# A hand-planned hybrid transformer block: new durations and ranks in the plan, and the gene norms of six batches turned by VectorE and a DRAM trip

## The chip, the core and the metric

The kernel runs on one core of a Trainium2 chip. The metric is the device time of one execution in microseconds (us). TensorE is called PE in the profile, with PEld for its weight loads; VectorE is DVE, ScalarE is ACT, GpSimd is POOL, and SyncE is SP, which here does nothing but issue DMAs. A profiled execution's span is the time from its first to its last instruction.

## The reference

Eight sequences (batches) of 256 tokens with 256 channels, all fp32, go through four residual layers, each after a layer norm:

```python
x = x + attn_a(_layernorm(x), Wqkv, Wout)          # 16 heads of 128, softmax over 256 keys
x = x + ffn(_layernorm(x), Wc, temperature, genes, Wd, Wu, norm_w, scale)
x = x + attn_b(_layernorm(x), w_q, w_k, w_v, w_o)  # 16 heads of 16, rope, block mask, causal
x = x + ffn(_layernorm(x), ...)                    # the same weights again

def ffn(x):
    xn = x * rsqrt(mean(x * x) + eps) * norm_w
    logits = einsum('btd,gd->btg', xn, Wc) / clip(temperature, 0.1)   # 512 genes
    top_vals, top_idx = top_k(logits, 32)
    expr_w = softmax(top_vals)
    expressed = einsum('btk,btkc->btc', expr_w, genes[top_idx])       # 32 wide
    down = tanh(expressed @ Wd.T); up = expressed @ Wu.T
    return down * xn * up * scale
```

The two `ffn` layers are called gene layers here.

## The kernel before

**Tiles and layers.** A batch is two tiles of 128 tokens, `xs[b, t]`, that stay in SBUF from the load to the store. The work of a batch is: attention A (`attn_a`, heads in pairs), layer 0 (the first gene layer, `ffn`), layer 1 (block attention, `attn_b`, one tile after the other), layer 2 (the second gene layer). Batch 7 takes attention A tile by tile (`attn_a_by_tile`) and its gene layers one tile at a time; the other batches run a gene layer for both tiles together. The batches do not depend on each other: while one batch is in its later layers, the next is in attention A.

**The plan.** No loop sets the order of instructions. Each operation is written down with `do(engine, (occ, lat), fn, pri, reads, writes, bufs)`: the time in ns for which it occupies its engine (`occ`), the time until its result is there (`lat`), a priority, the keys that it reads and writes, and the buffers that it holds. `Plan.order` (from line 135) then simulates the five engines: again and again it takes, of each engine, the operation with the smallest priority among those that can start within `WAIT[engine]` ns of the earliest one, and of these the one that starts first. The result is a static order for each engine, which the chip follows; real waits are by semaphores. In this simulation `HOP` is added where a result goes to another operation, `LOAD` more where PE reads it, `DRAIN` is in the latency of matmuls, and a DMA lands `FLIGHT` ns after its share of the queue, which is its size by `RATE` or `SCATTER`. A buffer comes free `HOP` ns after its last use. Where producer and user are on the same engine (SP excepted), the user may start when the producer's `occ` is over. `keep_warm` afterwards puts filler transposes into PE's gaps of more than 800 ns (line 1392 in the profile).

**Priorities.** Attention A of batch b has priorities from b to b + 1 (head by head; -0.5 for the norm on PE). For the other layers two tables hold a number for each batch, layer and tile: `PE_RANK` for PE and `EW_RANK` for VectorE, ScalarE, GpSimd and SP. A number such as 7.03 stands in the midst of batch 7's attention A; one of 20 and more is behind all of it; a negative one is ahead of all.

**Two ways to turn a matrix.** TensorE transposes 128 x 128 with the identity into a PSUM bank, and ScalarE copies the bank to SBUF. `turn` does it without these two: VectorE transposes 32 x 32 blocks into a tile `T` (line 510), SP writes `T` to a DRAM buffer `D` in four DMAs, and reads it back rearranged: with `flat=True` in four writes of 128-byte pieces (line 516) and four reads (line 526), otherwise four writes (line 519) and one read (line 528). The softmax weights of A (`PT`, used by the matmuls of line 721) and the A norms of batches 1 to 7 (`AxT`) go that way.

**The gene layer.** `ffn` calls `experts` for each tile: `normed` (statistics and scaling of the row, VectorE lines 461, 464 and 480, GpSimd lines 470 and 475) gives `Fxn`; two TensorE transposes (line 1054) and a ScalarE copy (line 1060) give `FxT`; the logits come from line 1068; four rounds of `max` (line 1078) and `match_replace` (line 1095) on VectorE mark the 32 largest; line 1100 makes the weights `Fe`, which are turned (by `turn` for batches 0 to 4, by TensorE at line 966 for the rest), multiplied with the genes (line 992) and with Wd and Wu (line 1012), and gated (lines 1025 to 1041). In `attn_b`, `Rxn` is turned at line 1134, line 1152 makes queries and keys, line 1228 scores, lines 1344 to 1361 softmax, line 1253 turns weights for batch 7, line 1292 multiplies with the values, line 1327 projects, and line 1334 adds to x. Tile 1 needs the keys and values of tile 0.

Of the kernel before, what the change touches and what calls it, by code (L numbers as in the profile page):

```python
# [16 lines left out]
B, S, DIM = 8, 256, 256  # L17
P = 128
# [14 lines left out]
    [[-0.88, -0.88], [-0.87, -0.87], [-0.86, -0.86]],  # L33
    [[-0.85, -0.85], [-0.84, -0.84], [-0.83, -0.83]],
    [[-0.82, -0.82], [7.03, -0.81], [8.72, -0.8]],
    [[7.78, -0.79], [8.7, -0.78], [7.32, -0.77]],
]
EW_RANK = [
    [[1.62, 1.49], [20.64, 2.07], [2.72, 20.2]],
    [[2.79, 3.31], [3.38, 3.19], [21.34, 1.84]],  # L40
    [[22, 4.66], [21.53, 22.1], [3.28, 4.32]],
    [[22.77, 23], [4.69, 23.1], [5.73, 23.2]],
    [[24.18, 5.62], [4.78, 23.98], [6.79, 4.31]],
    [[25.44, 6.57], [5.62, 7.27], [25.2, 7.37]],
    [[8.15, 6.17], [7.09, 26.01], [29.52, 26.55]],
    [[9.27, 8.68], [26.56, 26.64], [7.38, 9.82]],
]
# [25 lines left out]
class Plan:  # L73
# [3 lines left out]

    HOP = 65.0
    LOAD = 300.0
    DRAIN = 165.0  # L80
    FLIGHT = 2000.0
    RATE = 330.0
    SCATTER = 200.0
    OPEN = 8
    WAIT = {"PE": 50.0, "DVE": 50.0, "ACT": 100.0, "POOL": 200.0, "SP": 400.0}

# [42 lines left out]
    def order(self):  # L129
# [31 lines left out]
        while len(done) < len(self.ops):  # L161
# [26 lines left out]
            if o.eng == "SP":  # L188
                self.moved = max(self.moved, t) + o.lat
                end = self.moved + self.FLIGHT  # L190
                open_.append(end + self.HOP)
                open_.pop(0)
            else:
                end = t + o.lat
            for b in o.bufs:
                b.touch -= 1
                b.end = max(b.end, end)
                if not b.touch:
                    slots[b.tag].append((b.end + self.HOP, b.i))
                    self.taken.setdefault((b.tag, b.i), []).append((b.begin, b.end + self.HOP))  # L200
            for u in o.users:
                u = self.ops[u]
                same = u.eng == o.eng and o.eng != "SP"
                hop = self.HOP + (self.LOAD if u.eng == "PE" else 0.0)
                u.ready = max(u.ready, t + o.occ if same else end + hop)
                u.left -= 1
                if not u.left:
                    ready[u.eng].append(u)
# [30 lines left out]
def kernel(  # L239
# [44 lines left out]
    def dve(cols, half=False):  # L284
        occ = 70.0 + cols * (0.52 if half else 1.04)
        return occ, occ + 90.0

    def act(cols, ptr=False):
        occ = 60.0 + cols * 0.833 + (90.0 if ptr else 0.0)
        return occ, occ + 110.0  # L290

# [161 lines left out]
    def normed(b, t, who, ew, rms=False, xn=None, after=(), held=()):  # L453
# [6 lines left out]
        do(  # L460
            "DVE", (330, 420), lambda: [nc.vector.bn_stats(st(), x())],
            ew, [(x, 0), *((y, 0) for y in after)], [(st, 0)],
        )
        do("DVE", (90, 175), lambda: [nc.vector.bn_aggr(mv(), st())], ew, [(st, 0)], [(mv, 0)])


        m, a = (1.0 + RMS_EPS, LN_EPS * RMS_EPS) if rms else (1.0, LN_EPS)
        do(
            "POOL", (220, 270),
            lambda: [nc.gpsimd.tensor_scalar(rs(), mv()[:, 1:2], m, a, ALU.mult, ALU.add)],  # L470
            ew, [(mv, 0)], [(rs, 0)],
        )
        do(
            "POOL", (520, 560),
            lambda: [nc.gpsimd.tensor_tensor(rs(), rs(), mhalf, ALU.pow)],
# [18 lines left out]
    def turn(sources, dst, n, pri, keys, flat=False):  # L494
# [8 lines left out]
        for j, (p, view) in enumerate(sources):  # L503
            def out(j=j):
                t = T()[:, : 4 * w].rearrange("p (c h f) -> p h c f", c=4, h=len(sources))[:, j]
                return t

            do(
                "DVE", dve(n * P),
                lambda out=out, view=view: [nc.vector.transpose(*view(out()))],  # L510
                pri, [(q, 0) for q, _ in sources], [(T, j)],
            )
# [20 lines left out]
    def normed_a(b):  # L533
# [35 lines left out]
        if b:  # L569
            for i, (a_, b_, f_) in enumerate((  # L570
# [3 lines left out]
                do(  # L574
                    "POOL", (480.0, 530.0),
                    lambda i=i, a_=a_, b_=b_, f_=f_: [
# [319 lines left out]
    def softmax(sc, keys, p, n, k, who, ew):  # L896
# [9 lines left out]
        for i in range(n):  # L906
            do(
                "ACT", (155 + k * 0.83 + 92, 155 + k * 0.83 + 200),
                lambda i=i: [nc.scalar.activation(  # L909
                    p()[:, i, :], s3()[:, i, :], AF.Exp, bias=nm()[:, i : i + 1],  # L910
                    accum_out=sm()[:, i : i + 1])],
                ew, [*keys, (nm, 0)], [(p, ("e", i)), (sm, i)],
            )
        do(
            "DVE", (75, 165), lambda: [nc.vector.reciprocal(sm(), sm())],  # L915
            ew, [], [(sm, i) for i in range(n)],
# [20 lines left out]
    def ffn(b, ts_, layer):  # L937
# [7 lines left out]
        sms = [sb([P, 1], "Fsm", 6) for _ in ts_]  # L945
        for t, xn, e, sm in zip(ts_, xns, es, sms):
            experts(
                b, t, layer, lambda stage, t=t: pe(stage, t), xn, e, sm, xns, es, [xs[b, i] for i in ts_])
        away = n == 2 and b < B - 3
# [45 lines left out]

        cost = 730.0 if n == 2 else 505.0
        do(
# [10 lines left out]
        m = P // n  # L1008
        cost = 1140.0 if n == 2 else 858.0
        do(  # L1010
# [10 lines left out]
    def gated(b, t, ew, pg, down, up, xn, sm):  # L1021
# [6 lines left out]
        do(  # L1028
            "DVE", (390, 490),
            lambda: [nc.vector.scalar_tensor_tensor(  # L1030
# [3 lines left out]
        vec(  # L1034
            b, t, 256, (700, 740),
            lambda e: [e.tensor_tensor(up(), up(), down(), ALU.mult)],
            ew, [(down, 0)], [(up, 0)],
        )
        vec(
            b, t, 256, (690, 730),  # L1040
            lambda e: [e.tensor_tensor(x(), x(), up(), ALU.add)],
            ew, [(up, 0)], [(x, 0)],
        )

    def experts(b, t, layer, pe, xn, e, sm, xns, es, both):


        ew = first(b, t, layer)
        normed(b, t, "F", ew, True, xn, both, xns)
        xT = sb([P, DC, P], "FxT", 2)  # L1050
        pt = bank("B")
        do(
            "PE", (218.0, 218.0 + plan.DRAIN),
            lambda: (nc.tensor.transpose(pt()[:, ts(c, P)], xn()[:, ts(c, P)], ident)
                     for c in range(DC)),
            pe(0), [(xn, 0)], [(pt, 0)], [xT, *es],
        )
        do(
            "ACT", act(256),
            lambda: [nc.scalar.copy(xT().rearrange("p c q -> p (c q)"), pt()[:, :S])],  # L1060
            ew, [(pt, 0)], [(xT, 0)],
        )
        pl = bank("B")
        left = sb([P, G], "Fleft", 2)
        for c in range(DC):
            do(
                "PE", mm(512),
                lambda c=c: [nc.tensor.matmul(  # L1068
                    pl(), xT()[:, c, :], wcT[:, c, :], start=c == 0, stop=c == DC - 1)],
                pe(1), [(xT, 0), ("wcT",)], [(pl, 0)], [left, *es],  # L1070
            )
        m8 = [sb([P, 8], f"Fm8{r}", 2) for r in range(4)]
        nm = sb([P, 1], "Fnm", 2)
        for r in range(4):
            src, key = (pl, (pl, 0)) if r == 0 else (left, (left, 0))
            do(
                "DVE", (600 if r else 640, 740 if r else 760),
                lambda r=r, src=src: [nc.vector.max(m8[r](), src())],  # L1078
                ew, [key], [(m8[r], 0)],
            )  # L1080
            if r == 0:
                do(
                    "DVE", (55, 150),
                    lambda: [nc.vector.tensor_scalar(
# [3 lines left out]
                do(  # L1088
                    "ACT", (690, 800),
                    lambda: [nc.scalar.activation(e(), pl(), AF.Exp, bias=nm(), scale=rtemp)],  # L1090
                    ew, [(pl, 0), (nm, 0), ("rtemp",)], [(e, 0)],
                )
            do(
                "DVE", (672, 755),
                lambda r=r, src=src: [nc.vector.match_replace(left(), m8[r](), src(), TAKEN)],  # L1095
                ew, [(m8[r], 0), key], [(left, 0)],
            )
        do(
            "DVE", (720, 820),
            lambda: [nc.vector.scalar_tensor_tensor(  # L1100
                e(), left(), TAKEN, e(), ALU.is_equal, ALU.mult, accum_out=sm())],
            ew, [(left, 0)], [(e, 0), (sm, 0)],
        )
        do("DVE", (75, 165), lambda: [nc.vector.reciprocal(sm(), sm())], ew, [], [(sm, 0)])

# [14 lines left out]
    def attn_b(b, t):  # L1120
# [26 lines left out]
        for i, n in enumerate("qk"):  # L1147
# [11 lines left out]
        do(  # L1159
            "DVE", (620, 720),  # L1160
            lambda: [nc.vector.stream_shuffle(sh().rearrange("p c s -> p (c s)"), pq(), swap)],
# [9 lines left out]
        vec(  # L1171
            b, t, 512, (1235, 1280),
            lambda e: [e.tensor_tensor(
# [4 lines left out]
        vec(  # L1178
            b, t, 512, (1230, 1275),
            lambda e: [e.tensor_tensor(r(), r(), sh(), ALU.add)],  # L1180
# [3 lines left out]
        for par in range(2):  # L1184
            vec(
                b, t, 256, (460, 520),
                lambda e, par=par: [e.tensor_scalar(
# [25 lines left out]
        def scores(c, pT):  # L1213
# [7 lines left out]
            def emit():  # L1221
# [10 lines left out]
            do(  # L1232
                "PE", (1200.0, 1200.0 + plan.DRAIN), emit, pe(3),
                [(r, 0), *((kbuf, (tt, par)) for tt in range(t + 1) for par in range(2))],
# [3 lines left out]
            for g in range(NR):  # L1238
                sc, p = scs[g], ps_[g]
                do(  # L1240
                    "DVE", (n * 53 + 93, n * 53 + 180),
                    lambda sc=sc: [nc.vector.memset(
# [37 lines left out]
        def attend(cs_, pT):  # L1280
# [16 lines left out]

            cost = 1200.0 if n * len(cs_) == 2 else 650.0
            do(
# [38 lines left out]
    def softmax_b(sc, p, p3, n, k, ew):  # L1338
# [8 lines left out]
        for i in range(n):  # L1347
            do(
                "ACT", (155 + k * 0.83 + 92, 155 + k * 0.83 + 200),
                lambda i=i: [nc.scalar.activation(  # L1350
# [4 lines left out]
        do(  # L1355
            "DVE", (75, 165), lambda: [nc.vector.reciprocal(sm(), sm())],  # L1356
            ew, [], [(sm, i) for i in range(n)],
# [91 lines left out]
```

## Time and profile before

| | before |
|---|---|
| median of 3 runs | 959.45 us (958.21 to 959.88) |
| profiled execution | 960.78 us |
| its span | 959.0 us |
| first PE matmul starts | 5.0 us after the span's start |
| last PE matmul ends | 954.3 us |
| DVE busy 60 to 840 us | 594.86 us of 780 |
| DMA share of the span | 49.2% (queue of SP) |
| last attention A projection (line 876) starts | 881.9 us |

"Busy" is time in which an engine ran an instruction; matmuls are pipelined, so a busy PE is not PE at its peak. The idle time before an instruction is put down to what released it last.

The DMA issues of the two ways of `turn`, with KB each and the median us from issue to landing, are in the same part of the page as these lines:

```profile
D<-T SPq DMA_DIRECT2D x28, 64.0 KB, 3.1
AxT<-D SPq DMA_DIRECT2D x28, 64.0 KB, 2.2
```

### The profile page before, as it was taken

The page shows a single profiled execution, that of the slowest core. Times are in us where ns is not written, and L with a number is a line of the kernel's source. Part 1 is how long each engine was busy: PE and PEld are TensorE (multiplying, and loading weights), DVE is VectorE, ACT ScalarE, POOL GpSimd, SP SyncE. Part 2 cuts the span into 40 slices and gives each one's busy share as a digit, 9 for nine tenths or more (in the row PEclk, how much of TensorE's full clock was granted, in tenths as well). Part 3 has the DMA queues.
Part 4 walks back from the last instruction along what each step waited for, and adds up shares of the span by engine and source line. Part 5 has one row for each costly group of instructions (what it writes and reads, how often), then busy time and mean ns, then how long its engine had stood idle before and what let it go on. Part 6 is the DMA issues. An engine that isn't in the chain of part 4 may idle for free.

```text
span 959.0 us, 17226 instructions
## 1 busy us (share of the span) xinstructions
PE 919.5 (96%) x5815; PEld 737.7 (77%) x5815; DVE 703.6 (73%) x1716; ACT 468.0 (49%) x1550; POOL 404.4 (42%) x530
## 2 busy tenths in 40 slices
PE   7999999999999999999999999999999999999776
PEld 6878888887678777887678788877777877787564
DVE  2543484769967789669886884988788788868765
ACT  3534343754266544564455554465436643764461
POOL 4722224642176422662247343464237414743430
PEclk9999999999999999999999999999999999999989
DMA  9873333476337763485455746177525731550000
GB/s 324 248 209 94 110 106 115 123 221 173 111 111 200 202 166 105 131 231 174 135 143 171 200 133 190 44 208 216 148 67 163 211 106 40 147 173 1 6 7 12
DMA packets 109192, 136.09 MB, mean 142 GB/s; under 512 B 26288, under 2 KB 90416, under 8 KB 109104
## 3 DMA queue, kind: packets, MB, share of 16 engines
q1 hardware_dynamic: 109104, 134.99, 49.2%
q8 instruction: 46, 0.75, 0.3%
q14 instruction: 42, 0.34, 0.1%
HBM read 72.82 MB, written 62.13 MB: 141 GB/s over the span
## 4 chain that ended last, share of the span: by engine, by line
PE 56%; DVE 32%; issue 4%; DMA 3%; POOL 2%; ACT 2%; SPq 1%; DVEq 0%; ACTq 0%
PE ps L674 12%; DVE Fleft L1095 8%; DVE Fm L1078 7%; PE ps L696 7%; PE ps L721 6%; PE ps L595 5%; PE ps L743 5%; DVE T L510 4%; PE ps L1068 2%; PE ps L1228 2%; DMA D<-T 2%; PE ps L1152 2%; DVE Bnm L1344 2%; DVE Fe L1100 2%; PE ps L789 2%
## 5 line engine op out<-in xcount | busy, mean ns | idle before, releaser
L920 POOL TENSOR_TENSOR p<-p,Asm 128x512 f32<-128x512 f32 x128 | 135.1, 1058 | 266.0 <-DVE Asm L915 262.7
L674 PE MATMUL ps<-AxT,wqk 128*128 128x256 f32 x896 | 222.6, 382 | 0.2 <-ACT Fe L1090 0.2
L674 PEld LDWEIGHTS ps<-AxT,wqk 128*128 128x128 f32 x896 | 169.9, 191 | 26.6 <-issue 3.5
L909 ACT ACTIVATE p<-ps,Anm 128x256 f32<-128x256 f32 x256 | 119.5, 474 | 106.7 <-DVE Anm L903 97.1
L510 DVE STREAM_TRANSPOSE T<-p 128x512 f32<-128x512 f32 x202 | 133.4, 689 | 11.6 <-POOL p L920 7.6
L1361 POOL TENSOR_TENSOR p<-p,Bsm 128x512 f32<-128x512 f32 x96 | 99.1, 1047 | 84.6 <-DVE Bsm L1356 84.1
L903 DVE TENSOR_REDUCE Anm<-ps 128x2 f32<-128x512 f32 x128 | 86.4, 678 | 52.0 <-PE ps L696 49.3
L696 PE MATMUL ps<-Aqk 128*128 128x256 f32 x448 | 119.6, 382 | 1.4 <-ACT Aqk L683 0.9
L1350 ACT ACTIVATE p<-ps,Bnm 128x128 f32<-128x128 f32 (+1 forms) x256 | 105.4, 445 | 30.9 <-DVE Bnm L1344 23.5
L743 PE MATMUL ps<-woutT,Aao 128*128 128x256 f32 x448 | 111.0, 383 | 1.4 <-ACT Aao L731 1.0
L721 PE MATMUL ps<-PT,Av 128*128 128x256 f32 x448 | 108.5, 382 | 0.2 <-DMA PT<-D 0.2
L683 ACT ACTIVATE Aqk<-ps 128x512 f32<-128x512 f32 x112 | 66.9, 605 | 69.1 <-PE ps L674 68.5
L743 PEld LDWEIGHTS ps<-woutT,Aao 128*128 128x128 f32 x448 | 82.9, 190 | 21.7 <-issue 6.6
L721 PEld LDWEIGHTS ps<-PT,Av 128*128 128x128 f32 x448 | 83.7, 190 | 17.3 <-issue 4.3
L696 PEld LDWEIGHTS ps<-Aqk 128*128 128x128 f32 x448 | 83.1, 190 | 17.3 <-ACT Aqk L683 3.6
L595 PE MATMUL ps<-wv,Ax 128*128 128x256 f32 x224 | 66.7, 386 | 2.6 <-ACT Av L616 1.8
L1344 DVE TENSOR_REDUCE Bnm<-ps 128x2 f32<-128x512 f32 (+1 forms) x96 | 66.2, 690 | 2.7
L1078 DVE MAX8 Fm<-Fleft 128x8 f32<-128x512 f32 x96 | 66.4, 692 | 2.4
L1095 DVE MATCH_REPLACE8 Fleft<-Fm,Fleft 128x512 f32<-128x512 f32 x96 | 64.8, 675 | 0.0
L616 ACT COPY Av<-ps 128x256 f32<-128x256 f32 x108 | 40.6, 376 | 46.8 <-PE ps L595 46.5
L1068 PE MATMUL ps<-wcT,FxT 128*128 128x512 f32 x128 | 60.8, 601 | 0.0
L1350 ACT ACTIVATION_READ_ACCUMULATOR p<-ps,Bnm 128x1 f32 x256 | 58.6, 229 | 0.0
(130 smaller groups left out, 1405.6 us busy)
## 6 DMA issues: line engine op xcount, KB each, us to landing
D<-T SPq DMA_DIRECT2D x444, 128.0 KB, 2.6
PT<-D SPq DMA_DIRECT2D x111, 512.0 KB, 4.1
wqk<-in_wqkvT_dram SPq DMA_DIRECT2D x8, 512.0 KB, 9.7
x<-in_x_dram SPq DMA_DIRECT2D x16, 128.0 KB, 3.4
wv<-in_wqkvT_dram SPq DMA_DIRECT2D x4, 512.0 KB, 10.0
woutT<-in_woutT_dram SPq DMA_DIRECT2D x4, 512.0 KB, 10.6
out_dram<-x SPq DMA_DIRECT2D x16, 128.0 KB, 2.0
D<-T SPq DMA_DIRECT2D x28, 64.0 KB, 3.1
```

Of the source, the lines that this page charges most:

```text
L510: lambda out=out, view=view: [nc.vector.transpose(*view(out()))],
L595: lambda: [nc.tensor.matmul(dst(), a(), w_, start=start, stop=True, skip_group_check=not start)],
L674: lambda kind=kind, c=c: [nc.tensor.matmul(pq()[:, ts(kind, S)].rearrange("p (t q) -> p t q", t=TT), wA[kind, g][:, c, ts(i, DA)], xT.row( ...
L696: lambda t=t: [nc.tensor.matmul(sc()[:, ts(t, S)], qk()[:, 0, ts(t, P)], qk()[:, 1, :], start=True, stop=True)],
L721: lambda j=j, k=k, g=g, i=i: [nc.tensor.matmul(po()[:, ts(j, S)].rearrange("p (t g q) -> p t g q", t=TT, g=4), vs[g]()[:, AT[k, i // 2], t ...
L743: lambda t=t, h=h: [nc.tensor.matmul(py()[:, ts(t, DIM)], ao[h - h % 2]()[:, h % 2, ts(t, P)], woutT[:, h, :], start=h == hs[0], stop=h == ...
L909: lambda i=i: [nc.scalar.activation(p()[:, i, :], s3()[:, i, :], AF.Exp, bias=nm()[:, i : i + 1], accum_out=sm()[:, i : i + 1])],
L920: lambda: [nc.gpsimd.tensor_tensor(p(), p(), sm().unsqueeze(2).to_broadcast((P, n, k)), ALU.mult)],
L1078: lambda r=r, src=src: [nc.vector.max(m8[r](), src())],
L1095: lambda r=r, src=src: [nc.vector.match_replace(left(), m8[r](), src(), TAKEN)],
L1350: lambda i=i: [nc.scalar.activation(p3()[:, i, :], s3()[:, i, :], AF.Exp, bias=nm()[:, i : i + 1], accum_out=sm()[:, i : i + 1])],
L1361: lambda: [nc.gpsimd.tensor_tensor(p3(), p3(), sm().unsqueeze(2).to_broadcast((P, n, k)), ALU.mult)],
```

## The change

There are three parts. The plan's durations are replaced nearly throughout; the rule for a user on the producer's own engine now holds for PE alone, so that on the other engines it waits for the producer's end and a hop; `HOP` becomes a number for each engine, `FREE` takes its place where a buffer comes free, and `WAIT` becomes 1 ns for all but VectorE. Both rank tables are new in many places. And in `ffn`, for batches 0 to 5, both tiles are normed first and then turned together by `turn(..., flat=True)` into one buffer `FxT` of both tiles, in place of the TensorE transposes and ScalarE copies; batches 6 and 7 keep those. What is computed stays the same.

```diff
-    [[-0.85, -0.85], [-0.84, -0.84], [-0.83, -0.83]],
-    [[-0.82, -0.82], [7.03, -0.81], [8.72, -0.8]],
-    [[7.78, -0.79], [8.7, -0.78], [7.32, -0.77]],
+    [[-0.85, -0.85], [-0.84, -0.84], [7.63, 6.56]],
+    [[-0.82, -0.82], [-0.81, -0.81], [7.18, 8.48]],
+    [[-0.79, -0.79], [-0.78, -0.78], [9.75, 7.16]],
 ]
 EW_RANK = [
-    [[1.62, 1.49], [20.64, 2.07], [2.72, 20.2]],
+    [[20, 20], [1.14, 1.45], [0.24, 20.2]],
...
-    [[8.15, 6.17], [7.09, 26.01], [29.52, 26.55]],
-    [[9.27, 8.68], [26.56, 26.64], [7.38, 9.82]],
+    [[9, 26], [7.22, 26.1], [26.23, 8.63]],
+    [[27, 9.22], [7.63, 8.46], [9.27, 8.63]],
...
-    HOP = 65.0
-    LOAD = 300.0
+    HOP = {"PE": 60.0, "DVE": 35.0, "ACT": 60.0, "POOL": 79.0, "SP": 60.0}
+    FREE = 40.0
+    LOAD = 200.0
     DRAIN = 165.0
-    FLIGHT = 2000.0
+    FLIGHT = 1600.0
     RATE = 330.0
-    SCATTER = 200.0
+    SCATTER = 290.0
     OPEN = 8
-    WAIT = {"PE": 50.0, "DVE": 50.0, "ACT": 100.0, "POOL": 200.0, "SP": 400.0}
+    WAIT = {"PE": 1.0, "DVE": 100.0, "ACT": 1.0, "POOL": 1.0, "SP": 1.0}
...
-                same = u.eng == o.eng and o.eng != "SP"
-                hop = self.HOP + (self.LOAD if u.eng == "PE" else 0.0)
+                same = u.eng == o.eng == "PE"
+                hop = self.HOP[u.eng] + (self.LOAD if u.eng == "PE" else 0.0)
                 u.ready = max(u.ready, t + o.occ if same else end + hop)
...
     def dve(cols, half=False):
-        occ = 70.0 + cols * (0.52 if half else 1.04)
-        return occ, occ + 90.0
+        occ = 65.0 + cols * (0.52 if half else 1.04)
+        return occ, occ + 78.0
...
-        for t, xn, e, sm in zip(ts_, xns, es, sms):
+        by_trip = n == 2 and b < B - 2
+        xT = sb([P, TT, S], "FxT", 1)
+        for t, xn in zip(ts_, xns):
+            normed(b, t, "F", first(b, t, layer), True, xn, [xs[b, i] for i in ts_], xns)
+        if by_trip:
+            turn(
+                [(xn, lambda T, xn=xn: (
+                    T.rearrange("p c (k q) -> p k c q", k=DC),
+                    xn().rearrange("p (k c q) -> p k c q", k=DC, c=4))) for xn in xns],
+                lambda: xT().rearrange("p t s -> p (t s)"), DC, first(b, ts_[-1], layer),
+                [(xT, i) for i in range(n)], flat=True,
+            )
+        else:
+            for i, (t, xn) in enumerate(zip(ts_, xns)):
+                pt = bank("B")
+                do(
+                    "PE", (218.0, 218.0 + plan.DRAIN),
...
+                    pe(0, t), [(xn, 0)], [(pt, 0)], [xT, *es],
+                )
...
+        for i, (t, xn, e, sm) in enumerate(zip(ts_, xns, es, sms)):
             experts(
-                b, t, layer, lambda stage, t=t: pe(stage, t), xn, e, sm, xns, es, [xs[b, i] for i in ts_])
+                b, t, layer, lambda stage, t=t: pe(stage, t), (xT, i), lambda c, i=i: xT()[:, i, ts(c, P)], e, sm, es)
...
             do(
-                "DVE", (600 if r else 640, 740 if r else 760),
+                "DVE", (610, 690),
                 lambda r=r, src=src: [nc.vector.max(m8[r](), src())],
...
             do(
-                "DVE", (672, 755),
+                "DVE", (671, 753),
                 lambda r=r, src=src: [nc.vector.match_replace(left(), m8[r](), src(), TAKEN)],
```

The remaining lines of the diff replace further durations in the same manner, most by a few per cent.

## The prediction

> **What bounds the kernel now.** I read the page's busy shares first, then busy time by stage, then PE's own waits, then the chain of waits near the end, then the DMA issues.
>
> ```profile
> span 959.0 us, 17226 instructions
> PE 919.5 (96%) x5815; PEld 737.7 (77%) x5815; DVE 703.6 (73%) x1716; ACT 468.0 (49%) x1550; POOL 404.4 (42%) x530
> ```
>
> ```profile
> 60.00:840.00 780.00, 766.83 (x4763) 617.46 (x4762) 594.86 (x1439) 387.52 (x1300) 330.00 (x421) 1.00 0.52 148
> 840.00:900.00 60.00, 55.71 (x433) 43.56 (x434) 48.14 (x124) 28.46 (x86) 22.81 (x30) 1.00 0.22 65
> 900.00:959.00 59.00, 42.16 (x394) 32.27 (x392) 35.69 (x92) 26.26 (x91) 17.34 (x22) 0.92 0.03 10
> ```
>
> Columns of the second fence: stage, length, then busy time (instructions) of PE, PEld, DVE, ACT and POOL, the granted clock, DMA share, GB/s. TensorE sets the pace of the body: from 60 to 840 us it idles 780 - 766.83 = 13.2 us, at a granted clock of 1.00. VectorE is the next engine, at 594.86 / 780 = 76%. In the last 119 us PE idles 4.3 + 16.8 = 21.1 us, and 149 of its instructions there are fillers (line 1392), so the end is a chain and not a full engine.
>
> ```profile
> PE ps L966 <- DVE Fe L1100: 7.1, 8, 2.2
> PE ps L1134 <- DVE Rxn L480: 4.5, 5, 2.1
> PE ps L1054 <- DVE Fxn L480: 3.2, 4, 1.4
> PE ps L1253 <- POOL p L1361: 3.2, 4, 2.0
> PE ps L721 <- DMA PT<-D: 0.2, 1, 0.2
> ```
>
> These are PE's waits over the whole span (total, times, longest). They are for the ends of VectorE's chains; for a DRAM trip's landing PE waits 0.2 us in all. The DMA-queue trips therefore cost nothing today, and the transposes on PE do.
>
> **The change part by part.** I sum against the span of 959.0 us. The profiled execution took 960.78 us, 1.78 above its span; the median of the runs, 959.45, stands 0.45 above the span, and I add that at the end.
>
> *(a) 48 transposes leave PE.* Six batches (0 to 5), two gene layers, two tiles, two 128-column transposes each. A pair costs PE the step from its start to the next instruction's:
>
> ```profile
> 328.23 0.38 PE L1054 MATMUL ps<-ident,Fxn 128*128 128x128 f32 x2
> 328.45 1.03 PE L721 MATMUL ps<-PT,Av 128*128 128x256 f32 x4
> ```
>
> 0.22 us for two, so 24 pairs x 0.22 = 5.3 us off a full engine. The waits in front of them go too: 0.8 us from 60 to 840 us (PE's idle time there before line 1054 that Fxn ended). I take -6.1; the bounds are -6.1 and 0 (the freed time becomes a wait elsewhere). ScalarE loses 24 copies of 0.38 us (line 1060), and 24 uses of a PSUM bank go with them; at 49% busy ScalarE sets nothing, so I cost that at nothing.
>
> *(b) Twelve DRAM trips come instead.* Each is two VectorE transposes, four writes and four reads on SP's queue, the way that the A norms already go. VectorE: 24 x 0.419 us (the mean of the 14 transposes T<-Axn) = 10.1 us, which raises its share by one point; PE's work covers it, and if that cover is gone it is at most +10.1 on the end. SP: each write is in the queue 0.63 us and each read 0.42 us (medians of lines 516 and 526), 48 x 0.63 + 48 x 0.42 = 50 us over the first 800 or so. All SP issues now add up to about 305 us of 959, so the queue has room; but it is in order, and reads of PT for heads stand behind a write that waits on VectorE (205 us of SP's waits are of that kind). The latency of a trip rises: from the start of the first T<-Axn to the last landing I read 8.6 to 13.2 us in three A trips, against 0.22 + 0.38 us of work through PE. What covers it is the next batch's A heads, which do not need this batch's gene result. With it hidden I take 0; the bounds are 0 and 12 x 1.05 = +12.6 (the mean of the four waits of VectorE for a T buffer, 4.2 us in all, paid once by each trip).
>
> The Trainium skill, page "VectorE: DVE Perf Modes", section "Rules for kernel authors", speaks against this part: for a full 128x128 transpose it names TensorE where a PSUM destination is acceptable, since VectorE turns only 32x32 blocks. The rows above agree on latency, 0.6 us of work against some 9 us of trip; by that rule taken as a cost on the path, the sum would be 12 x 8 = 96 us worse, and by the rows, which show a busy PE and no PE wait for trips, 6.1 us better.
>
> *(c) The plan's durations.* The static order is made from these numbers. One step matters most: before, an operation on the same engine could follow when the producer's slot ended; now it waits for the result and a hop. The trace, in the chain of waits:
>
> ```profile
> 876.44 0.70 DVE Fm L1078
> 877.17 0.76 DVE Fleft L1095 x2
> 877.96 0.71 DVE Fm L1078
> ```
>
> A round of top-k takes 877.96 - 876.44 = 1.52 us. The old plan allowed 0.640 + 0.672 = 1.31, the new one 0.690 + 0.035 + 0.753 + 0.035 = 1.51. Over four rounds the old plan had the result Fe some 0.8 us too early, and PE's largest wait is for Fe (7.1 us, 8 times). So the old order puts PE at such places before the data; the new one would fill in other work first. At most the whole idle time of the body goes, 13.2 us less the 0.8 of (a) = 12.4; at least none. As the greatest named waits are of this kind but not all, I take about half, -6.4.
>
> *(d) The plan's DMA times go the other way.* Page rows:
>
> ```profile
> D<-T SPq DMA_DIRECT2D x444, 128.0 KB, 2.6
> PT<-D SPq DMA_DIRECT2D x111, 512.0 KB, 4.1
> ```
>
> Four writes are issued within 1.31 us (the median from first to fourth), so an undisturbed head trip takes 1.31 + 2.6 + 4.1 = 8.0 us. The old constants give 4 x 0.655 + 2.0, a hop of 0.065, then 2.62 + 2.0 = 9.3 us. The new give 4 x 0.452 + 1.6, a hop of 0.06, then 1.81 + 1.6 = 6.9 us: 1.1 short of the trace, and 2.4 us earlier than the old plan. PE's load margin falls by 0.1 as well. So PE meets its L721 matmuls 2.5 us earlier relative to the landing. For the 56 head pairs before, I took the time from the last landing of a PT read to the pair's first L721 matmul: median 3.0 us, lower quartile 1.6. In 22 of the 56 it is under 2.5, and the shortfalls add up to 26.9 us. That is the upper bound; the lower is 0. A wait of PE delays all that follows and so gives the other trips in flight their time back, and SP, whose window of choice goes from 400 to 1 ns, should send reads with fewer detours (a read now issues 5.8 us after its first write by the median, though the writes have landed after 4.2). I take a quarter, +6.7.
>
> *(e) The end.* Batch 7's block attention gets ranks 7.63 and 8.46 where it had 26.56 and 26.64, so it goes ahead of batch 6's last gene layer (tile 0 26.23 and tile 1 8.63, before 29.52 and 26.55). On the chain of waits the top-k of one such tile lies from 872.69 to 880.29 us, 7.6 us. I take half of it, -4; the bounds are -8 (all of it) and +10 (rival 3).
>
> The other parts (the ranks of early batches, FREE, POOL's costs) change the order where PE is full either way, and have no row of their own; they are inside (c). One buffer FxT for both tiles in place of two half as large costs nothing where gene layers lie apart: pairs of Fxn stand 10 us and more apart, and a tile needs it some 3 us until its logits.
>
> Sum: 959.0 - 6.1 + 0 - 6.4 + 6.7 - 4 = 949.2; plus 0.45 = 949.7, so **950 us**.
>
> **The rivals.** 1. *Only the transposes count*: PE gains (a) and the rest cancels, 959.0 - 6.1 + 0.45 = 953.4. For it: PE is full, and its body floor hardly moves. Against: six named waits that the durations speak to.
>
> 2. *The trips are counted too short, and PE waits for landings* (slower): the wait that is 0.2 us now takes the place of those removed, at line 721. Price: all of 26.9 us, against gains of (a) and (c): 959.0 - 6.1 - 6.4 + 26.9 + 0.45 = 973.9. It decides from where more than 6.1 + 6.4 = 12.5 us are paid, about half. For it: the plan's own 6.9 against 8.0 us. Against: waits in a pipeline of several trips are not added up one by one.
>
> 3. *The end is late* (slower): batch 7's first gene layer of tile 0 gets rank 27, behind everything else on VectorE, and tile 1's block attention needs that tile's keys. If its top-k (7.6 us) and the norm, reciprocal and gating around it (some 2.4 us by rows of 0.16 to 0.48) fall behind the last A head, the end moves by +10; with the rest of (c) and (d) at their values, 949.2 + 4 + 10 + 0.45 = 963.7. Against: VectorE idles 60 - 48.1 = 11.9 us from 840 to 900, where such low work still finds its place.
>
> 4. *No change*: gains and the DMA shortfall cancel within 0.2%, 1.9 us (about what a measurement of this kernel can tell from no change).
>
> **How the numbers follow.** Chances: the forecast 0.46, rival 1 0.17, rival 2 0.20, rival 3 0.11, no change 0.06. Faster 0.46 + 0.17 = 0.63, same 0.06, slower 0.31. The forecast's own range goes from all of (a), (c) and the end's -8 with no DMA wait, 959.0 - 6.1 - 12.4 - 8 + 0.45 = 933, to 956. The range of 8 in 10 adds rival 3 and the lower half of rival 2: 933 to 970.
>
> **What would show it.** Right: no L1054 matmul for batches 0 to 5 (16 left of 64), 24 more T transposes of 128x256, PE waits on Fe, Rxn and Fxn in the body under 6 us, PE's idle time from 60 to 840 at 7 to 14 us, part of it now on landings of PT or FxT. Rival 2: waits of PE or PEld for PT<-D or FxT<-D of over 12 us in all. Rival 3: the top-k of batch 7's first layer, tile 0, after the last L876. The prediction is wrong if VectorE, not PE, is full in the body (over 85% from 60 to 840), or if the time from the last L876 to the end is over 90 us (77 now).

## The result

The changed kernel takes 989.29 us (median of 4 runs, 986.16 to 989.67) against 958.83 us for the kernel before in the same comparison: a ratio of 1.0309, 95% interval 1.0286 to 1.0333, so 3.1% slower. The forecast was 950 us. The profiled execution took 989.36 us with a span of 987.6 us, 28.6 us more than the 959.0 before.

### The profile page after: what moved, and what is told of

Read it like the earlier page. It is cut to its first block, busy times and chain, and to the rows that moved or that the text cites. A ratio compares the mean times of both kernels' runs of the same rounds, so it can differ in the third digit from the quotient of the medians.

```text
span 987.6 us, 17304 instructions
## 1 busy us (share of the span) xinstructions
PE 921.5 (93%) x5748; PEld 731.3 (74%) x5748; DVE 685.7 (69%) x1740; ACT 462.2 (47%) x1526; POOL 403.5 (41%) x530
## 2 busy tenths in 40 slices
DMA packets 136841, 142.38 MB, mean 144 GB/s; under 512 B 52401, under 2 KB 116529, under 8 KB 136753
## 3 DMA queue, kind: packets, MB, share of 16 engines
q1 hardware_dynamic: 136752, 141.29, 50.7%
## 4 chain that ended last, share of the span: by engine, by line
PE 42%; DMA 21%; DVE 19%; SPq 7%; issue 4%; ACT 3%; POOL 3%; DVEq 0%; ACTq 0%; POOLq 0%
DMA PT<-D 10%; DMA D<-T 9%; PE ps L675 7%; PE ps L744 5%; PE ps L722 5%; SPq L520 4%; PE ps L1082 4%; DVE T L511 4%; PE ps L697 4%; DVE Fleft L1109 4%; PE ps L596 3%; DVE Fm L1092 3%; PE ps L1166 2%; DMA FxT<-D 2%; DVE Anm L904 1%
## 5 line engine op out<-in xcount | busy, mean ns | idle before, releaser
L722 PE MATMUL ps<-PT,Av 128*128 128x256 f32 x448 | 112.9, 392 | 18.1 <-DMA PT<-D 16.6
L697 PEld LDWEIGHTS ps<-Aqk 128*128 128x128 f32 x448 | 83.9, 190 | 16.4 <-issue 4.3
L732 ACT COPY Aao<-ps 128x512 f32<-128x512 f32 x56 | 33.0, 593 | 76.8 <-PE ps L722 76.4
L1092 DVE MAX8 Fm<-Fleft 128x8 f32<-128x512 f32 x96 | 64.2, 683 | 0.5
L1358 DVE TENSOR_REDUCE Bnm<-ps 128x2 f32<-128x512 f32 (+1 forms) x96 | 62.2, 665 | 0.1
```

Source lines behind the costliest of these rows:

```text
L697: lambda t=t: [nc.tensor.matmul(sc()[:, ts(t, S)], qk()[:, 0, ts(t, P)], qk()[:, 1, :], start=True, stop=True)],
L722: lambda j=j, k=k, g=g, i=i: [nc.tensor.matmul(po()[:, ts(j, S)].rearrange("p (t g q) -> p t g q", t=TT, g=4), vs[g]()[:, AT[k, i // 2], t ...
```

## The profile after

The page's busy shares, and then busy time by stage (stage, length, PE, PEld, DVE, ACT, POOL, clock, DMA share, GB/s):

```profile
span 987.6 us, 17304 instructions
PE 921.5 (93%) x5748; PEld 731.3 (74%) x5748; DVE 685.7 (69%) x1740; ACT 462.2 (47%) x1526; POOL 403.5 (41%) x530
...
PE 42%; DMA 21%; DVE 19%; SPq 7%; issue 4%; ACT 3%; POOL 3%; DVEq 0%; ACTq 0%; POOLq 0%
```

```profile
60.00:840.00 780.00, 735.80 (x4395) 584.50 (x4393) 546.34 (x1371) 359.83 (x1194) 303.74 (x391) 0.99 0.54 150
840.00:900.00 60.00, 59.40 (x462) 50.55 (x462) 45.49 (x121) 37.37 (x130) 34.29 (x41) 1.00 0.29 85
900.00:987.60 87.60, 71.93 (x667) 52.56 (x665) 67.77 (x185) 40.04 (x131) 32.35 (x43) 0.99 0.12 36
```

From 60 to 840 us PE now idles 780 - 735.8 = 44.2 us, where it idled 13.2. PE's idle time in the whole span grew from 39.5 to 66.1 us, by 26.6 of the 28.6. The granted clock is hardly the cause: over the whole span it is 0.994, where it was 0.995. The last line of the first fence is the chain of waits by engine: DMA has 21% of it and SP's queue 7%, where they had 3% and 1% in the same line of the kernel before:

```profile
PE 56%; DVE 32%; issue 4%; DMA 3%; POOL 2%; ACT 2%; SPq 1%; DVEq 0%; ACTq 0%
```

PE's waits by what ended them (total, times, longest) say which transfers:

```profile
PE ps L722 <- DMA PT<-D: 16.6, 19, 2.1
PE ps L1082 <- DMA FxT<-D: 8.9, 8, 2.7
PE ps L1306 <- DMA PT<-D: 8.1, 10, 1.8
PE ps L1020 <- DMA PT<-D: 5.1, 5, 1.8
...
PE ps L965 <- DVE Fxn L481: 1.9, 3, 0.7
...
PE ps L994 <- DVE Fe L1114: 1.4, 2, 1.0
```

Lines 722, 1306, 1020 and 1082 of the changed kernel are the value matmuls of attention A, those of block attention, the gene sums and the logits (before: 721, 1292, 992 and 1068). PE waited 0.2 us in all for landings before; now the first four lines alone make 38.7 us, and with a wait of 0.6 at line 860 it is 39.3. The waits for the ends of VectorE's chains went the other way: Fe 7.1 to 1.4 us, Fxn 3.2 to 1.9. The transfers themselves are hardly slower: writes of 128 KB land after 2.8 us in place of 2.6, those of 64 KB after 2.3 in place of 3.1.

```profile
D<-T SPq DMA_DIRECT2D x444, 128.0 KB, 2.8
PT<-D SPq DMA_DIRECT2D x111, 512.0 KB, 4.1
D<-T SPq DMA_DIRECT2D x76, 64.0 KB, 2.3
...
FxT<-D SPq DMA_DIRECT2D x48, 64.0 KB, 2.3
```

PT lands 4.1 us after its issue, as before, and a PT trip from the first write's issue to the landing of the read takes 9.3 us by the median (9.8 before). What changed is where PE stands in its program when the data land. From the landing of a head pair's own PT read to the first matmul of its values there were 3.4 us by the median before, and under 2.5 in 15 of the 56 pairs; now it is 0.2 us, and under 2.5 in 51. (The prediction measured from the latest landing of any PT read, which is often another pair's; by that the median before was 3.0.)

## The experiments

The theory after the result (L): the plan counts trips too short, so the order puts PE at its reads before the landings, and PE pays. Rivals: the new order (ranks, greedy choice) is bad by itself (O); VectorE's waits for a free T tile drive it (T; 4.2 us before, 37.5 now); the trip of the gene norms is the cost (D). The wait that T means is, in the changed kernel:

```profile
DVE T L511 <- DMA D<-T: 37.5, 24, 4.0
```

### 1. The same order without the waits

`after_no_landing_wait` keeps the order of the instructions of the changed kernel and takes PE's reason to wait away: the matmuls read a constant. (Dots mark lines left out; batch 7's attention A has the same replacement.)

```diff
+    still = woutT[:, :HG, :].rearrange("p h m -> p (h m)")
...
-                            pT().rearrange("p h f -> p (h f)").rearrange(
+                            still.rearrange(
                                 "p (g h k t q) -> p h k t g q", g=4, h=2, k=TT, t=TT)[:, j, k],
...
-                return wT().rearrange("p h f -> p (h f)").rearrange(
+                return still.rearrange(
...
-            return pT[g // 2]().rearrange("p h f -> p (h f)").rearrange(
+            return still.rearrange(
...
-                b, t, layer, lambda stage, t=t: pe(stage, t), (xT, i), lambda c, i=i: xT()[:, i, ts(c, P)], e, sm, es)
+                b, t, layer, lambda stage, t=t: pe(stage, t), (xT, i), lambda c, i=i: still[:, ds(i * S + c * P, P)] if by_trip else xT()[:, i, ts(c, P)], e, sm, es)
```

> The order of every engine's instructions is that of the changed kernel; only the matmuls that read a turned matrix which came back by a DRAM trip (PT of attention A, of the gene weights and of block attention, and FxT of batches 0 to 5) read the constant weights woutT instead, so TensorE never waits for these landings (the trips still run; the result leaves out what they bring). Theory L (the plan counts trips too short and PE pays the landings, 16.6 + 8.9 + 8.1 + 5.1 = 38.7 us of waits in the changed kernel): 945 to 960 us. Rival O (the new order is worse by itself: ranks, greedy choice, and the waits on landings only stand where others would): 975 to 989 us. Rival T (VectorE's waits for a free T tile, 37.5 us, drive it): 970 to 985 us, and these waits stay.

Measured: 948.15 us, ratio 0.988 (0.986 to 0.9899) to the kernel before; the span is 947.6 us, 40.0 less than that of the changed kernel. In this trace 34 of the 56 head pairs start their value matmuls before their own PT has landed, by up to 3.6 us; the median pair starts 0.5 us before. The control makes the same replacement in the kernel before:

> Control: the same replacement in the kernel before, whose PE waits for trips' landings are 0.2 us at line 721 and little elsewhere (the trips still run; the result leaves out what they bring). Theory L: 955 to 960 us, as before. If it falls by more than 1%, the replacement itself makes the kernel faster and the other run can't be read as the price of landings.

Measured: 959.92 us, ratio 1.0002 (0.9993 to 1.0012). So the replacement by itself is worth nothing in the kernel before, and the waits for landings cost the changed kernel 40 us; without them its order is 1.2% faster than the one before. The replacement has one more effect: SP may refill a PT tile without waiting for the matmuls that read it. SP's waits for PE at the PT reads are 7.4 us in the changed kernel and 11.2 in the kernel before, where taking them away gained nothing, so this is hardly the 40 us. Of these 40 us, 28.2 are idle time of PE (66.1 to 37.9 us) and 11.8 busy time (921.5 to 909.7); what makes up the second part was not traced. Rival O falls. Rival T falls too: the wait of VectorE for a T tile grew from 37.5 us to this, while the time fell:

```profile
DVE T L511 <- DMA D<-T: 46.0, 27, 4.0
```

### 2. Part of the waits

`after_A_only` makes the replacement for attention A alone, `after_FxT_only` for the logits alone.

> The changed kernel's order; only attention A's value matmuls (batches 0 to 7 where the weights came by a trip) read the constant woutT in place of PT, so that PE's waits for these landings (16.6 us at line 722) are gone and the others (FxT 8.9, block attention 8.1, genes 5.1) stay. Theory L with waits that add up: about 987.6 - 17 = 971 us of span, 968 to 975 in time. Rival (the waits absorb each other, so that the others grow into the room): 978 to 988 us, with FxT and the other PT waits over 28 us in sum, against 22.1 now.

Measured: 975.0 us (ratio 1.0152, 1.0136 to 1.0167), 14.3 less than the changed kernel; the profiled execution, the fastest of four, has a span of 971.2, 16.4 less. The 16.6 us of waits at line 722 are gone. The other landing waits grew from 22.1 us to 30.5, which is the rival's sign (over 28), but the time did not stay at the rival's 978 to 988:

```profile
PE ps L1306 <- DMA PT<-D: 14.8, 14, 2.9
PE ps L1082 <- DMA FxT<-D: 9.2, 7, 2.0
PE ps L1020 <- DMA PT<-D: 6.5, 6, 1.6
```

> The changed kernel's order; only the logits of batches 0 to 5 read the constant woutT in place of FxT (the logits are not the reference's there), so PE does not wait for the new trips of this change. Theory L, waits add up: 987.6 - 8.9 in span, 977 to 982 us in time. If the trips of this change were the main cause: 950 to 965 us. If absorbed: 985 to 989 us.

Measured: 979.56 us (1.0211, 1.0194 to 1.0228), 9.7 less than the changed kernel for 8.9 us of removed waits; the profiled execution, again the fastest of four, has a span of 974.9, 12.7 less. Attention A's waits stay (18.0 us at line 722). The waits for the trips that this change added are thus a quarter to a third of the 40 us; the rest is at trips that were there before. By the medians, each removal shortens the time by about the waits that it removes. The two add up to 24 of the 41 us between the medians of the changed kernel and of `after_no_landing_wait`; block attention and the gene weights, with 13.2 us of waits, were not tried by themselves.

### 3. One number of the plan

```diff
-    FLIGHT = 1600.0
+    FLIGHT = 2400.0
```

> The changed kernel with one number changed: FLIGHT 2400 in place of 1600, so that the plan counts a head's trip as 4 x 0.45 + 2.4 + 0.06 + 1.81 + 2.4 = 8.5 us (8.0 by the undisturbed rows of the trace). The order is a new one, with the ranks as they are. Theory L: PE's waits for landings fall from 38.7 us to under 8 and the time to 945 to 965 us, below the kernel before if the ranks still suit. Rival O (ranks and greedy choice are at fault): 970 us or more with few landing waits.

Measured: 947.25 us, ratio 0.9867 (0.9852 to 0.9881), span 946.9: as fast as the order without waits, with all work done. PE's landing waits are 9.2 us in all, a little more than the 8 that were expected:

```profile
PE ps L722 <- DMA PT<-D: 7.4, 6, 2.3
...
PE ps L1082 <- DMA FxT<-D: 1.0, 2, 0.7
...
PE ps L1306 <- DMA PT<-D: 0.6, 2, 0.3
```

The reverse, two numbers of the change in the kernel before:

```diff
-    FLIGHT = 2000.0
+    FLIGHT = 1600.0
...
-    SCATTER = 200.0
+    SCATTER = 290.0
```

> The kernel before with two numbers of the change alone: FLIGHT 1600 and SCATTER 290. Theory L: PE's waits for landings, 2 us at most before, rise to 15 us or more (no FxT trips here) and the time to 975 to 1000 us. Rival: it stays at 960 to 972, as for the order that came of a 50 ns change (971.7), with under 5 us of landing waits.

Measured in one run: 1003.92 us, more than the range given. There are 25.9 us of landing waits, where this kernel had 0.2:

```profile
PE ps L721 <- DMA PT<-D: 12.6, 13, 1.6
PE ps L1292 <- DMA PT<-D: 7.9, 9, 1.8
...
PE ps L992 <- DMA PT<-D: 4.3, 6, 1.2
```

25.9 us of waits do not make the 42 us by which the span grew. The rest is another effect, which the next two runs show.

### 4. How much an order is worth by chance

> The kernel before with FLIGHT 2050 in place of 2000, a change of 50 ns in what the plan believes and of nothing else. It measures how much a new order is worth by chance. Theory L alone: 955 to 963 us. If the ranks fit only the constants that they were found with: over 965 us with no more waits on landings.

Measured in one run: 971.69 us, with no landing wait of PE at all. 50 ns in one number of the plan cost 12 us: the ranks fit the constants with which they were found.

> The kernel before, its plan's durations, rule and ranks untouched, with only the DRAM trip of the gene norms of batches 0 to 5. Theory L: the old plan's long DMA times cover the trip, PE's landing waits stay under 5 us, and the 48 transposes are saved: 952 to 960 us. Rival O in a stronger form (ranks fit one set of operations only, any new plan scatters): over 965 us with few landing waits. Rival D (the trips themselves cost, on SP and VectorE): over 965 us with waits on FxT<-D.

Measured in one run: 1016.26 us, a miss for theory L taken alone: landing waits are 2.0 us. New operations in the old plan spoil its order as well: the ranks had been found without them. The filler transposes show it: 509 of them, where the kernel before has 163 and `before_flight_2050` 266. A filler stands only where the plan itself sees a gap of PE of over 800 ns.

So there are two effects, and the plan's own end (the time at which its simulation has the last DMA through), which follows from its arithmetic and not from the chip, separates them. To its left in the table is `FLIGHT` / `SCATTER`; the surplus is the measured span less the plan's end; the last column is all of PE's waits on landings.

| kernel | FLIGHT / SCATTER | plan's end us | span us | surplus us | landing waits us |
|---|---|---|---|---|---|
| before | 2000 / 200 | 926.8 | 959.0 | 32.2 | 0.2 |
| before_flight_2050 | 2050 / 200 | 943.9 | 969.8 | 25.9 | 0 |
| before_plus_trip | 2000 / 200 | 983.7 | 1014.4 | 30.7 | 2.0 |
| before_new_dma_times | 1600 / 290 | 940.8 | 1001.1 | 60.3 | 25.9 |
| after | 1600 / 290 | 915.4 | 987.6 | 72.2 | 39.3 |
| after_no_landing_wait | 1600 / 290 | 915.4 | 947.6 | 32.2 | 0 |
| after_flight_2200 | 2200 / 290 | 946.3 | 975.3 | 29.0 | 7.1 |
| after_flight_2400 | 2400 / 290 | 920.2 | 946.9 | 26.7 | 9.2 |

Where the plan's DMA times are long enough, the chip takes 26 to 32 us more than the plan says; with 1600 / 290 it takes 60 to 72, and 32.2 again when PE does not wait for landings. `after_flight_2200` was made to try this split:

> The changed kernel with FLIGHT 2200 and its own ranks; the plan's own end is 946.3 us, by chance of the order. Theory L has two parts, the plan's end and the landings that it does not see: few landing waits (under 15 us) and 972 to 980 us. A rival in which FLIGHT alone sets the time, in between 1600 (989) and 2400 (947): 955 to 960 us.

Measured in one run: 977.05 us, as the two parts say, and not between its neighbours at 1600 and 2400.

### 5. Ranks found anew, with the trip of the gene norms and without

With `FLIGHT = 2400` I searched ranks by the plan's own end, twice with the trip (`refit_trip`) and three times with `by_trip = False`, that is with the transposes of TensorE. Ranks apart, both have the first of these edits to the changed kernel, and the form without the trip has the second too:

```diff
-    FLIGHT = 1600.0
+    FLIGHT = 2400.0
...
-        by_trip = n == 2 and b < B - 2
+        by_trip = False
```

> The changed kernel with FLIGHT 2400 and with ranks found anew for that number (the plan's own end falls from 920.2 to 916.4 us). In the kernels whose DMA times are long enough the chip took 26 to 32 us of span more than the plan's own end (926.8 to 959.0, 943.9 to 969.8, 983.7 to 1014.4, 920.2 to 946.9). Theory L with that rule: 942 to 949 us. Rival (the ranks fit a model that is too fine, the surplus grows with the fitting): 950 to 970 us.

> The same with FLIGHT 2400, but the gene norms of all batches turned by TensorE as before, and ranks found anew for that (the plan's own end is 920.8 us). If the trip of the gene norms saves what its 48 transposes take, this is 3 to 7 us slower than refit_trip: 946 to 953 us. If the trip gives nothing: equal within 2 us.

Measured: 948.8 us with the trip (0.9865, 0.9826 to 0.9903) and 942.07 without (0.9806, 0.9786 to 0.9825), the reverse of the plan's ends, 916.4 and 920.8, and outside both of the ranges given for the second. Whether that was a cost of the trip or one draw of an order, further sets were to tell:

> As refit_trip, with a second set of ranks found on its own (the plan's own end 916.2 us, 916.4 there). If the trip costs more than its transposes save: 946 to 952 us, as refit_trip (948.8). If the difference to refit_no_trip (942.1) was chance of the ranks: 938 to 945 us.

> As refit_no_trip, with a second set of ranks (the plan's own end 921.1 us, 920.8 there). If orders without the trip run closer to their plan: 939 to 945 us, 4 us or more below both kernels with the trip. If chance: 946 us or more.

> A third set without the trip (the plan's own end 921.1 us). As for refit_no_trip_2: 939 to 945 us, or 946 and more if chance.

Measured: 942.34 us with the trip (0.981, 0.9792 to 0.9829); without it 942.83 (0.983, 0.980 to 0.986) and 941.84 (0.9816, 0.9791 to 0.9841). So the 6.7 us between the first two were for the most part the chance of the first set with the trip. The spans are 947.3 and 941.7 us with the trip, and 938.8, 939.5 and 939.1 without; the surpluses over the plan are 30.9 and 25.5 us with it, and 18.0, 18.4 and 18.0 without. The plan promises 4 to 5 us for the trip; in these two sets with it and three without, the chip gives none of it. What of a trip the plan misses was not tried by itself, so the cause stays open. The rows offer two candidates: PE's landing waits, 9.5 and 9.4 us with the trip and 1.7 to 4.3 without, and SP's queue, where a write of 64 KB is 0.63 us (the median of line 517) and the plan counts 0.44.

## Why the prediction was wrong

**The bound** was read rightly: PE sets the pace of the body. It was also right that PE paid nothing for landings in the kernel before.

**Step (d) failed: its cost.** It found the mechanism, that PE meets line 721's matmuls "2.5 us earlier relative to the landing". But it took "a quarter, +6.7", on the ground that a wait of PE gives the other trips in flight their time back. The runs show such relief only in part: without attention A's waits the other landing waits grew by 8.4 us, and still the time fell by 14.3 us for 16.6 us of waits; removing all waits took 40.0 us off the span. So the waits are paid nearly in full. The term also summed only attention A's trips. Those of block attention, of the gene weights and of the gene norms added 8.1 + 5.1 + 8.9 = 22.1 us of waits. The term measures +40.0 us, from 947.6 to 987.6, in place of +6.7. Two of its readings were off as well. Its bound of 26.9 us was taken from the latest landing of any PT read; from each pair's own read, told by the order of reads and matmuls in the plan, the same sum is 14.6 us, so attention A's 16.6 us went past it. And the shift is larger than 2.5 us: where PE does not wait, the median pair is 0.5 us ahead of its landing, and it was 3.4 us behind it before, 3.9 us in all.

**Rival 2** named what happened, with its row (line 721, PT) and its sign (waits for landings of over 12 us), but its 973.9 us counts attention A's trips alone, as (d) does, and its chance of 0.20 was too small.

**Step (a)**: 16 transposes of Fxn are left of 64, and 24 of VectorE came, as counted:

```profile
L511 DVE STREAM_TRANSPOSE T<-Fxn 128x256 f32<-128x256 f32 x24 | 9.5, 425 | 2.9 <-DMA D<-T 2.7
```

PE lost 48 x 0.109 = 5.2 us of work (0.109 us from one transpose's start to the next), but with ranks found for each form this shows in no time. **Step (b)** priced the trip at 0, and it is not hidden whole: without PE's waits for it the changed kernel took 9.7 us less. The page "VectorE: DVE Perf Modes" of the Trainium skill, section "Rules for kernel authors", which names TensorE for a 128x128 transpose, was weighed against the rows and put aside; the runs of section 5 bear it out for this kernel to the extent that TensorE's way is no slower.

**Step (c)** cannot be shown to have come as priced. Without landing waits the span is 11.4 us shorter than before. Of this, 9.8 us are busy time of PE (919.5 to 909.7): 5.2 of the transposes, some 2 of fillers (144 in place of 163), the rest not traced. Only 1.6 us are idle time (39.5 to 37.9), where (c) had taken 6.4, and from 60 to 840 us PE idles 780 - 762.96 = 17.0 us, in place of 13.2:

```profile
60.00:840.00 780.00, 762.96 (x4695) 618.10 (x4694) 570.46 (x1440) 379.68 (x1271) 324.65 (x417) 1.00 0.54 154
```

Its named waits did fall: those for Fe, Rxn and Fxn from 14.8 to 5.6 us. But others grew, such as this one (0.8 us before):

```profile
PE ps L596 <- DVE Av L608: 5.7, 3, 2.4
```

Its reading of the old plan was a little off too: 0.640 us stood for the first `max` alone and 0.600 for the other three, so Fe came some 0.95 us earlier in the plan than on the chip, not 0.8.

**Step (e)** did not come: from the start of the last projection of attention A to the end it takes 76.3 us, where it took 77.1 and 4 us less were expected. **Rival 3** did not come either, for the same number. **Rival 1** and **no change** fall with the 40 us. Without (d) the sum is 942.5 us of span; the order without waits measured 947.6.

The best version is the changed plan with `FLIGHT = 2400`, ranks found for it, and the gene norms left on TensorE: 941.84 to 942.83 us in three sets of ranks, 1.7% to 1.9% under the kernel before, and with the trip 942.34 in the better of two sets.

## What to carry to other kernels

In this static order, a latency that was counted too short was paid on the engine that is full, nearly in full and at every place that reads it. Counted at 8.5 us (8.0 by the undisturbed rows, 9.3 by the median trip of the changed kernel) in place of 6.9, it lengthened the plan by 4.8 us and shortened the kernel by 42. So when durations in a planner are replaced, compare each with the trace as a whole path (issue, landing, read, landing), and look at how much margin the present order leaves between landing and use. Ranks fit the constants that they were found with and are best found anew for others: here 50 ns in one constant moved the time by 1.3%.

## What the runs showed of the hardware that was not expected

Writes of 64 KB in 128-byte pieces land no later and no sooner than those of 128 KB with any regularity. Their median is 3.1 us in the kernel before (28 writes, 2.6 us for 128 KB), 2.3 in the changed kernel (76 writes from 2.1 to 5.0, 2.8 for 128 KB), and 2.3 to 3.4 in the kernels with ranks found anew. The 26,113 small packets more (52,401 under 512 B, 26,288 before) raised the queue's share of the DMA engines only from 49.2% to 50.7%, of a span that is 3% longer: from 472 to 501 us, 2.4 us for each of the twelve trips. The added trips thus take little of the DMA engines' time; what PE waits for is their latency.
